# Layer 1's feed-forward in a small vision tower: scores and values of two steps in one run each, value products by column halves

## The chip, the cores and the metric
One core of a Trainium2 chip runs the whole program. The metric is the device time of one execution in microseconds, the median of the runs.

## What is computed
The reference is a tower of two layers over 32 images of 3 x 256 x 256: a tokenizer (16 x 16 patches, 256 tokens of 256 features per image), then per layer an attention and a feed-forward, each behind a layer norm and added to the stream. The change lies in layer 1's feed-forward, which is itself a small attention with experts. For every image, with 4 heads `n`, 4 experts `e`, 64 features per head and s = 256 tokens:

```
sx = x @ hl_w.T + hl_b                          # 4 heads of 64 features
q[n,e] = sx[n] @ wq[n,e].T ; k[n] = sx[n] @ wk[n].T ; v[n] = sx[n] @ wv[n].T
att[n,e] = softmax(q[n,e] @ k[n].T * 8 + causal)
out[n,e] = att[n,e] @ v[n]
gs[n] = softmax over e of (out[n,:] flattened @ gate_w[n].T + gate_b[n])
mixed[n] = sum over e of gs[n,e] * out[n,e]
h = layernorm(mixed + resid) ; y = layernorm(relu(h @ fc1.T + b1) @ fc2.T + b2 + h)
result = y * softmax over heads of (y @ fgate_w.T)
```

Everything is float32.

## The kernel before
The stages (tokenizer, layer 0 attention, layer 0 feed-forward, layer 1 attention, layer 1 feed-forward) run one after the other over all images; the 32 images' streams `H` stay on the chip. All matrix products write one of 8 PSUM banks of 512 columns, handed out in turn by `bank()`; every product goes through the helper `mm` (L113), so in the profile nearly all have that line and are told apart by their tiles. Each product shows there as two passes, each with a weight load (PEld).

In the last stage `A` holds wq and wk multiplied into each other, so that scores need `g = A.T sx` and `sx` alone; `WV` holds wv beside four small blocks, one per expert, that carry the values through `gate_w`, and `ones_row` adds a column of ones to each block, which yields the softmax's denominator. An image goes through pieces:

- `prep` 0 to 5: normalize and transpose (`ex`, `exT`), `sx` (weights `hl`), `g` for head pairs 0 and 1 (products `sx,A`, 64 x 64 tiles of the array, two heads side by side), the values `ev` (weights `WV`), a tile for the output `eo`.
- six score steps k (head pair k // 3, part k % 3). `scores` makes two products `g,sx` of 512 columns, one per head, on 64-row tiles; `weights` adds the triangular mask to the bank (VectorE, L825) and writes the exponential into `et` (ScalarE, L828).
- six value steps. For a head and a half of the tokens, `values` multiplies `et` (128 x 128 as weights) with the head's 84 columns of `ev` for each expert, into one bank of 4 x 84 columns, and ScalarE copies it to `eo` (L839). In the second half of the tokens there are two products per expert.
- `post` 0 to 13: reciprocal of the denominators, gate logits, softmax over the experts, `eo` times `gate` on GpSimd (L888), the sum over the experts (`two`, `er`, VectorE L893 to L896), a norm (`ss` on VectorE, `hv` by a power on GpSimd L844 and L845, the product L906), transposes into `fxT`, `fc1`, `fc2` and `centre`, a second norm (`ey`), transposes into `foT`, `fo_w`, the gate over heads (`fgate`) and `fout`, which is sent to memory.

A time step `t` enters an image every 6 steps, so up to five images are in hand. Within a step the order written is: scores, posts, preps, mask and exponential, values. So TensorE's stream has, in each of the six steps of a lap, one score run of 4 passes, then products on the full array, then one value run of 16 passes. Each engine takes its queue in order; waits between the queues are semaphores.

## Time and profile before
| | |
|---|---|
| median of 3 runs | 2424.4 us (2422.5 to 2426.04) |
| the profiled execution | 2421.16 us, span 2419.4 us |
| mean granted TensorE clock | 0.983 |
| busy share of the span | PE 97%, PEld 70%, DVE 57%, ACT 35%, POOL 21% |
| starts of `eo` on POOL (L888), images 3 to 30 | 30.03 to 30.05 us apart |

PE is TensorE's matrix passes, PEld its weight loads, DVE VectorE, ACT ScalarE, POOL GpSimd. Passes overlap in the array, so their lengths are modelled; the distance between starts is the better measure. An idle time in brackets behind a row names what ended it.

### The profile page before, as it was taken

What the parts mean: (1) busy time and instruction counts of PE and PEld (TensorE: products, weight loads), DVE (VectorE), ACT (ScalarE), POOL (GpSimd) and SP (SyncE); (2) the same over time, 40 slices, a digit from 0 to 9 for tenths busy, and PEclk for the clock granted to TensorE, in tenths of its full rate; (3) what the DMA queues carried; (4) which work ended last, traced back from release to release, by engine and by line L of the source; (5) the groups of instructions that cost most, each with busy time, mean ns of one, the idle gap of its engine ahead of it and who ended that gap; (6) DMA issues with size and microseconds to landing.
All of it is one profiled execution on the core that took longest, in us unless ns stands there. A gap on an engine that the chain in (4) does not pass through costs nothing.

```text
span 2419.4 us, 30697 instructions
## 1 busy us (share of the span) xinstructions
PE 2337.0 (97%) x12062; PEld 1681.9 (70%) x12062; DVE 1387.6 (57%) x3769; ACT 850.2 (35%) x1543; POOL 517.2 (21%) x461
## 2 busy tenths in 40 slices
PE   8999999999979999999999999999999999999995
PEld 6885666666656776766676667777777777777774
DVE  2435333333366665455465555777777777777775
ACT  0003222222202122144344444555555555555552
POOL 0002122221122121143233102222222222222222
PEclk9999999999989999999899999999999999999997
DMA  7420000000010000000000000000000000000000
GB/s 281 146 98 1 0 1 1 0 1 1 0 38 1 1 1 1 1 1 1 1 1 1 1 1 1 10 10 10 10 10 10 10 10 10 10 10 10 10 10 19
DMA packets 25895, 44.32 MB, mean 18 GB/s; under 512 B 1936, under 2 KB 11408, under 8 KB 25360
## 3 DMA queue, kind: packets, MB, share of 16 engines
q1 hardware_dynamic: 23872, 36.00, 4.3%
q10 hardware_dynamic: 1872, 6.29, 0.7%
q8 instruction: 97, 1.59, 0.3%
q14 instruction: 54, 0.44, 0.1%
HBM read 33.90 MB, written 8.39 MB: 17 GB/s over the span
## 4 chain that ended last, share of the span: by engine, by line
PE 91%; DVE 4%; ACT 1%; DMA 1%; POOL 1%; issue 1%; SPq 0%; DVEq 0%; ACTq 0%; POOLq 0%
PE bank L113 86%; PE bank L481 2%; PE bank L186 1%; DMA patch<-in_patches_dram 1%; PE bank L946 1%; POOL hv L845 1%; PE bank L947 1%; ACT bxT L191 0%; DVE cx L172 0%; POOL eo L888 0%; ACT et L828 0%; PE bank L539 0%; PE bank L586 0%; DVE bank L825 0%; DVE fout L960 0%
## 5 line engine op out<-in xcount | busy, mean ns | idle before, releaser
L113 PEld LDWEIGHTS bank<-ev,et 128*128 128x128 f32 x3072 | 361.2, 192 | 28.5 <-issue 11.7
L113 PE MATMUL bank<-ev,et 128*128 128x84 f32 x3072 | 373.7, 275 | 0.0
L828 ACT ACTIVATE et<-bank 128x512 f32<-128x512 f32 x384 | 222.3, 597 | 345.1 <-DVE bank L825 344.4
L113 PE MATMUL bank<-g,sx 64*128 64x512 f32 x768 | 216.9, 641 | 0.0
L825 DVE TENSOR_TENSOR bank<-bank,w_tri 128x256 f32<-128x256 f32 (+1 forms) x384 | 185.4, 514 | 52.2 <-PE bank L113 52.2
L888 POOL TENSOR_TENSOR eo<-eo,gate 128x2048 f32<-128x2048 f32 x32 | 115.8, 3620 | 394.5 <-DVE gate L886 394.5
L113 PE MATMUL bank<-w_tokW,patch 128*128 128x256 f32 x768 | 168.7, 384 | 11.9 <-DMA patch<-in_patches_dram 11.8
L113 PEld LDWEIGHTS bank<-w_tokW,patch 128*128 128x128 f32 x768 | 147.9, 193 | 32.3 <-DMA patch<-in_patches_dram 12.3
L113 PE MATMUL bank<-bxT,w_wuv 128*128 128x512 f32 x320 | 146.9, 598 | 4.9 <-ACT bxT L191 4.8
L839 ACT COPY eo<-bank 128x336 f32<-128x336 f32 x256 | 109.9, 444 | 98.5 <-PE bank L113 97.6
L332 DVE TENSOR_TENSOR bv<-bank,rows_b 128x512 f32<-128x512 f32 x64 | 44.3, 692 | 157.9 <-PE bank L113 157.9
L113 PE MATMUL bank<-sx,A 64*64 64x256 f32 x1024 | 124.3, 383 | 0.6 <-ACT sx L771 0.6
L113 PE MATMUL bank<-w_w,hT 128*128 128x256 f32 x512 | 115.8, 380 | 0.0
L113 PE MATMUL bank<-xsel,w_w 128*128 128x512 f32 x256 | 114.2, 600 | 0.0
L113 PE MATMUL bank<-w_wo,gT 128*128 128x256 f32 x512 | 113.1, 380 | 0.0
L113 PE MATMUL bank<-attn,bv 128*128 128x256 f32 x512 | 113.1, 380 | 0.0
L113 PE MATMUL bank<-w_wuv,bxT 128*128 128x512 f32 x256 | 112.5, 593 | 0.0
L113 PEld LDWEIGHTS bank<-attn,bv 128*128 128x128 f32 x512 | 97.5, 191 | 19.4 <-issue 7.2
L113 PEld LDWEIGHTS bank<-w_wo,gT 128*128 128x128 f32 x512 | 97.5, 191 | 13.0
L845 POOL TENSOR_TENSOR hv<-hv,minus_half 128x8 f32<-128x8 f32 x64 | 104.7, 1636 | 5.3
L113 PEld LDWEIGHTS bank<-bxT,w_wuv 128*128 128x128 f32 x320 | 59.5, 190 | 65.1 <-issue 53.6
L113 PEld LDWEIGHTS bank<-w_w,hT 128*128 128x128 f32 x512 | 95.7, 191 | 12.2 <-issue 0.5
(238 smaller groups left out, 3974.3 us busy)
## 6 DMA issues: line engine op xcount, KB each, us to landing
patch<-in_patches_dram SPq DMA_DIRECT2D x16, 1536.0 KB, 6.4
out_dram<-fout SPq DMA_DIRECT2D x32, 256.0 KB, 2.1
w_w<-in_w_dram ACTq DMA_DIRECT2D x2, 1024.0 KB, 13.4
w_wuv<-in_wuv_dram ACTq DMA_DIRECT2D x1, 1152.0 KB, 13.7
w_tokW<-in_tokW_dram ACTq DMA_DIRECT2D x1, 768.0 KB, 7.5
w_wo<-in_wo_dram ACTq DMA_DIRECT2D x1, 512.0 KB, 16.3
rows_b<-in_rows_b_dram ACTq DMA_DIRECT2D x1, 384.5 KB, 14.8
rows_e<-in_rows_e_dram ACTq DMA_DIRECT2D x1, 296.0 KB, 4.1
```

The lines of the kernel that those rows point to most:

```text
L113: nc.tensor.matmul(o, lhsT, rhs, start=first, stop=last)
L186: nc.tensor.transpose(p[:, o : o + P], x[:, c, k * P : (k + 1) * P], ident)
L332: nc.vector.tensor_tensor(v, p, row_b("b_v"), ALU.add)
L481: nc.tensor.transpose(p[:, o : o + P], x[:, c, k * P : (k + 1) * P], ident)
L825: nc.vector.tensor_tensor(own, own, over(tri, [P, n_e, P], 1), ALU.add)
L828: nc.scalar.activation(t.rearrange("p e n -> p (e n)"), p, AF.Exp)
L839: nc.scalar.copy(im.o[:, c * NH + n, 0 : NE * VC], p[:, 0 : NE * VC])
L845: nc.gpsimd.tensor_tensor(v, v, minus_half, ALU.pow)
L888: nc.gpsimd.tensor_tensor(im.by_e, im.by_e, over(im.gate, [P, NC * NH, NE, HD], 3), ALU.mult)
L946: nc.tensor.matmul(p[:, 0 : P + NH], im.fT[:, 0, s], fo_w[:, 0, :], start=True, stop=True)
L947: nc.tensor.matmul(p[:, P : 2 * P + NH], im.fT[:, 1, s], fo_w[:, 1, :], start=False, stop=True, skip_group_check=True,)
```

## The change
Four things change, all in this stage.

`A` becomes block-diagonal over the two heads of a pair (128 x 128 with zeros off the blocks), and the products `sx,A` run on the full array, one for two heads.

The columns of a head's values are laid out as experts 0 and 1's gate blocks, the 64 values, experts 2 and 3's blocks, so that an expert needs only a window of 74, 69, 69 or 74 columns of the 84. A value product is made by column halves: 64 of the 128 weight columns each, into partitions 0 to 63 and 64 to 127 of the bank.

The steps are paired. On even steps the scores of steps k and k+1 follow each other (8 passes); on odd steps a third of an image's values (64 half-width passes). Mask and exponential of k come on the even step, those of k+1 on the odd one.

The posts are spread over 19 steps instead of 14 in a table, and an image takes 34 steps instead of 29. Where `eo` was read as one view over four experts it is now two views of two, so the reciprocal, the gate logits and GpSimd's product are two instructions each; GpSimd's are half as long in elements.

```diff
-    VC = HD + NE * (NE + 1)
-    OC = NE * (VC + NE + 1)
+    EC = NE + 1
+    VC = NE * EC + HD
+    TAKE = ((0, 2 * EC + HD), (EC, EC + HD), (2 * EC, EC + HD), (2 * EC, 2 * EC + HD))
+    OC = sum(w for _, w in TAKE)
...
-    A = pwe.tile([P, 2, NE, HD], F32, name="A")
+    A = pwe.tile([P, 2, NE, P], F32, name="A")
...
                     for e in range(2):
-                        for h in range(2):
-                            s = slice(h * HD, (h + 1) * HD)
-                            mm(p[s, e * N : (e + 1) * N], A[s, hp, 2 * j + e, :], im.sx[s, hp, :])
+                        mm(p[:, e * N : (e + 1) * N], A[:, hp, 2 * j + e, :], im.sx[:, hp, :])
...
         def values(im, j):
-            hp, part = j // 3, j % 3
-            for n, c in (((2 * hp, 0), (2 * hp + 1, 0)), ((2 * hp, 1),), ((2 * hp + 1, 1),))[part]:
+            for n, c in (((0, 0), (1, 0), (0, 1)), ((1, 1), (2, 0), (3, 0)), ((2, 1), (3, 1)))[j]:
                 p = bank()
                 t0, t1 = im.t[n]
+                o = 0
                 for e in range(NE):
+                    x, w = n * VC + TAKE[e][0], TAKE[e][1]
                     for m in range(c + 1):
                         t = t1[:, e, :] if m else t0[:, e, c * P : (c + 1) * P]
-                        mm(p[:, e * VC : (e + 1) * VC], t, im.v[:, m, n * VC : (n + 1) * VC], m == 0, m == c)
-                nc.scalar.copy(im.o[:, c * NH + n, 0 : NE * VC], p[:, 0 : NE * VC])
+                        for q in (slice(0, HD), slice(HD, P)):
+                            mm(p[q, o : o + w], t[:, q], im.v[:, m, x : x + w], m == 0, m == c)
+                    o += w
+                nc.scalar.copy(im.o[:, c * NH + n, 0:OC], p[:, 0:OC])
...
-                nc.gpsimd.tensor_tensor(
-                    im.by_e, im.by_e, over(im.gate, [P, NC * NH, NE, HD], 3), ALU.mult
-                )
+                im.mix = [expert_pair(im, k, MIX, HD) for k in range(2)]
+                for k in range(2):
+                    nc.gpsimd.tensor_tensor(
+                        im.mix[k], im.mix[k], over(im.gate[:, :, 2 * k : 2 * k + 2], [P, NC * NH, 2, HD], 3), ALU.mult
+                    )
...
-        PREP, POST = 6, 15
+        SCORES, VALUES = 6, 9
+        POST = {15: 0, 16: 1, 17: 2, 19: 3, 20: 4, 21: 5, 22: 6, 23: 7, 27: 8, 28: 9, 29: 10, 30: 11, 32: 12, 33: 13}
...
+            if t % 2:
+                weigh()
+            else:
+                for b, i in active:
+                    if SCORES <= i < SCORES + 6:
+                        scores(images[b], i - SCORES)
+                        scores(images[b], i - SCORES + 1)
             for b, i in active:
-                if i >= POST:
-                    post(b, images[b], i - POST)
+                if i in POST:
+                    post(b, images[b], POST[i])
             for b, i in active:
-                if i < PREP:
-                    prep(b, images[b], i)
...
+                prep(b, images[b], i)
+            if t % 2:
+                for b, i in active:
+                    if VALUES <= i < VALUES + 6:
+                        values(images[b], (i - VALUES) // 2)
+            else:
+                weigh()
```

The framework reorders instructions within a queue when the program is built. In the built program of the changed kernel a lap (6 steps) stands in this order on each queue, by tiles; several images are mixed:

```
PE    fc1; values, third 2; scores 0 and 1; transposes of ey; A, pair 1; transposes of ex; WV;
      values, third 3; scores 2 and 3; fo_w; hl (sx); fc2 and centre; values, third 1;
      scores 4 and 5; transposes of er; A, pair 0
DVE   mask 0 (2), mask 1 (2); copy g; ex (2); ev (2); rden (2), lg, good, mask 2, good, lg, mask 2;
      gate sum, mask 3, gate softmax with mask 3 and the fgate copies between, gate last product;
      fgate, fout (8); two; ey; er, er; ss; mask 4; good; ey x hv; mask 4; ss; mask 5 (2); good;
      er x hv; junk (2); copy g
ACT   exp 0 (2), exp 1, foT, exp 1; copy g; copy exT; eo (2); exp 2 (2), exp 3, gate exp, exp 3,
      fgate exp; sx (2); eo (2); square of ey; eo; square of er; exp 4 (2), exp 5, fxT, copy g,
      exp 5; hx; eo (3)
POOL  eo x gate in two halves; hv of ey (2); hv of er (2)
```

`two` waits for POOL's second half, `ey x hv` and `er x hv` for `hv`, and `fc1` for `fxT`.

More of the change, by code (lines that the diff above doesn't have):

```diff
@@ L372, in vit_tower @@
     LOW, HIGH, MOST = 1e-28, 1e28, 1e37
-    VC = HD + NE * (NE + 1)
-    OC = NE * (VC + NE + 1)
+    EC = NE + 1
+    VC = NE * EC + HD
+    TAKE = ((0, 2 * EC + HD), (EC, EC + HD), (2 * EC, EC + HD), (2 * EC, 2 * EC + HD))
+    OC = sum(w for _, w in TAKE)
+    starts = [sum(w for _, w in TAKE[:e]) for e in range(NE)]
+    OWN = [starts[e] + (0, EC, 2 * EC + HD, 3 * EC + HD)[e] - TAKE[e][0] for e in range(NE)]
+    MIX = [starts[e] + 2 * EC - TAKE[e][0] for e in range(NE)]
     right_e, right_d, passing = ExitStack(), ExitStack(), ExitStack()
@@ L438, in prepare @@
             nc.vector.tensor_scalar(wo1[:, k, :], wo1[:, k, :], col("ln_w", k), None, ALU.mult)
-        for t in (WV, ones_row, fc2):
+        for t in (A, WV, ones_row, fc2):
             nc.gpsimd.memset(t, 0.0)
-        nc.gpsimd.memset(
-            ones_row.rearrange("p (n x) -> p n x", n=NH)[:, :, HD:VC]
-            .rearrange("p n (e x) -> p n e x", e=NE)[:, :, :, NE : NE + 1], 1.0,
-        )
+        for n in range(NH):
+            for o in (NE, EC + NE, 2 * EC + HD + NE, 3 * EC + HD + NE):
+                nc.gpsimd.memset(ones_row[:, n * VC + o : n * VC + o + 1], 1.0)
         nc.vector.tensor_copy(fo_w[:, 0, 0:P], ident)
@@ L460, in prepare @@
                 mm(pv[s, hp * 16 : hp * 16 + 16], wv_o[s, hp, :], gw_d[s, hp, :])
-        nc.scalar.mul(A.rearrange("p h e d -> p (h e d)"), pa, math.sqrt(HD))
         for i in range(2):
             s = slice(i * HD, (i + 1) * HD)
+            nc.scalar.mul(A[s, :, :, s], pa[s].rearrange("p (h e d) -> p h e d", h=2, e=NE), math.sqrt(HD))
             nc.vector.tensor_copy(fc2[s, s], f2[s, :])
@@ L467, in prepare @@
                 w = WV[s, hp, i * VC : (i + 1) * VC]
-                nc.vector.tensor_copy(w[:, 0:HD], wv_i[s, hp, :])
-                nc.vector.tensor_copy(
-                    w[:, HD:].rearrange("p (e x) -> p e x", e=NE)[:, :, 0:NE],
-                    pv[s, hp * 16 : hp * 16 + 16].rearrange("p (e x) -> p e x", e=NE),
-                )
+                nc.vector.tensor_copy(w[:, 2 * EC : 2 * EC + HD], wv_i[s, hp, :])
+                for k, o in enumerate((0, 2 * EC + HD)):
+                    nc.vector.tensor_copy(
+                        w[:, o : o + 2 * EC].rearrange("p (e x) -> p e x", e=2)[:, :, 0:NE],
+                        pv[s, hp * 16 + k * 8 : hp * 16 + k * 8 + 8].rearrange("p (e x) -> p e x", e=2),
+                    )
     def feature_major(x):
@@ L756, in vit_tower, with __init__ @@
         class Image:
-            pass
+            def __init__(self):
+                self.p, self.t = {}, {}
         G8 = [P, NC * NH, HD]
@@ L763, in prep @@
                 im.xT = features(p2, b)
-            if i == 1:
+            if i == 2:
                 im.sx = p2.tile([P, 2, N], F32, name="sx")
@@ L774, in prep @@
                 im.g = p2.tile([P, 2, NE, N], F32, name="g")
-            if i in (2, 3):
-                hp = i - 2
+            if i in (4, 6):
+                hp = i // 2 - 2
                 for j in range(2):
@@ L779, in prep @@
                     for e in range(2):
-                        for h in range(2):
-                            s = slice(h * HD, (h + 1) * HD)
-                            mm(p[s, e * N : (e + 1) * N], A[s, hp, 2 * j + e, :], im.sx[s, hp, :])
+                        mm(p[:, e * N : (e + 1) * N], A[:, hp, 2 * j + e, :], im.sx[:, hp, :])
                     copy_split(j, im.g[:, hp, 2 * j : 2 * j + 2, :].rearrange("p e n -> p (e n)"), p)
-            if i == 4:
+            if i == 7:
                 im.v = p2.tile([P, NC, NH * VC], F32, name="ev")
@@ L796, in prep @@
                 )
-            if i == 5:
-                im.o = p2.tile([P, NC * NH, OC], F32, name="eo")
+                im.o = p2.tile([P, NC * NH, 360], F32, name="eo")
         def scores(im, k):
@@ L804, in scores @@
             if part == 0:
-                im.t = getattr(im, "t", {})
                 for h in range(2):
@@ L809, in scores @@
                     )
-            im.p = []
+            im.p[k] = []
             for h in range(2):
@@ L816, in scores @@
                     mm(p, im.sx[s, hp, P:N], im.g[s, hp, :, P:N])
-                im.p.append(p)
+                im.p[k].append(p)
         def weights(im, k):
@@ L822, in weights @@
             for h in range(2):
-                p, n_e = im.p[h], 4 if part == 2 else 2
+                p, n_e = im.p[k][h], 4 if part == 2 else 2
                 own = p.rearrange("p (e n) -> p e n", e=n_e)[:, :, 0:P]
@@ L865, in squares, with expert_pair @@
             return sq
+        def expert_pair(im, k, at, w):
+            x, step = at[2 * k], at[2 * k + 1] - at[2 * k]
+            return im.o[:, :, x : x + 2 * step].rearrange("p g (e x) -> p g e x", e=2)[:, :, :, 0:w]
         def post(b, im, i):
             if i == 0:
-                by_e = im.o.rearrange("p g (e x) -> p g e x", e=NE)
                 im.rden = spool.tile([P, NC * NH, NE], F32, name="rden")
-                nc.vector.reciprocal(im.rden, by_e[:, :, :, HD + NE])
+                lg = spool.tile([P, NC * NH, NE, NE], F32, name="lg")
+                own = [expert_pair(im, k, OWN, EC) for k in range(2)]
+                for k in range(2):
+                    nc.vector.reciprocal(im.rden[:, :, 2 * k : 2 * k + 2], own[k][:, :, :, NE])
                 nc.vector.scalar_tensor_tensor(good, im.rden, 1.0 / LOW, good, ALU.is_le, ALU.mult)
                 nc.vector.scalar_tensor_tensor(good, im.rden, 1.0 / HIGH, good, ALU.is_ge, ALU.mult)
-                lg = spool.tile([P, NC * NH, NE, NE], F32, name="lg")
-                nc.vector.tensor_tensor(
-                    lg, by_e[:, :, :, HD : HD + NE], over(im.rden, [P, NC * NH, NE, NE], 3), ALU.mult
-                )
+                for k in range(2):
+                    e = slice(2 * k, 2 * k + 2)
+                    nc.vector.tensor_tensor(
+                        lg[:, :, e, :], own[k][:, :, :, 0:NE], over(im.rden[:, :, e], [P, NC * NH, 2, NE], 3), ALU.mult
+                    )
                 im.gate = spool.tile([P, NC * NH, NE], F32, name="gate")
@@ L886, in post @@
                 nc.vector.tensor_tensor(im.gate, im.gate, im.rden, ALU.mult)
-                im.by_e = im.o[:, :, 0 : NE * VC].rearrange("p g (e x) -> p g e x", e=NE)[:, :, :, 0:HD]
-                nc.gpsimd.tensor_tensor(
-                    im.by_e, im.by_e, over(im.gate, [P, NC * NH, NE, HD], 3), ALU.mult
-                )
+                im.mix = [expert_pair(im, k, MIX, HD) for k in range(2)]
+                for k in range(2):
+                    nc.gpsimd.tensor_tensor(
+                        im.mix[k], im.mix[k], over(im.gate[:, :, 2 * k : 2 * k + 2], [P, NC * NH, 2, HD], 3), ALU.mult
+                    )
             if i == 3:
                 two = p1.tile([P, NC * NH, 2, HD], F32, name="two")
-                nc.vector.tensor_tensor(two, im.by_e[:, :, 0:2, :], im.by_e[:, :, 2:4, :], ALU.add)
+                nc.vector.tensor_tensor(two, im.mix[0], im.mix[1], ALU.add)
                 im.r = p2.tile(G8, F32, name="er")
@@ L968, in vit_tower, with weigh @@
         images = [Image() for _ in range(B)]
-        PREP, POST = 6, 15
-        for t in range(6 * (B - 1) + POST + 14):
-            active = [(b, t - 6 * b) for b in range(B) if 0 <= t - 6 * b < POST + 14]
+        SCORES, VALUES = 6, 9
+        POST = {15: 0, 16: 1, 17: 2, 19: 3, 20: 4, 21: 5, 22: 6, 23: 7, 27: 8, 28: 9, 29: 10, 30: 11, 32: 12, 33: 13}
+        for t in range(6 * (B - 1) + 34):
+            active = [(b, t - 6 * b) for b in range(B) if 0 <= t - 6 * b < 34]
+            def weigh():
+                for b, i in active:
+                    if SCORES <= i < SCORES + 6:
+                        weights(images[b], i - SCORES)
+            if t % 2:
+                weigh()
+            else:
+                for b, i in active:
+                    if SCORES <= i < SCORES + 6:
+                        scores(images[b], i - SCORES)
+                        scores(images[b], i - SCORES + 1)
             for b, i in active:
-                if PREP <= i < PREP + 6:
-                    scores(images[b], i - PREP)
+                if i in POST:
+                    post(b, images[b], POST[i])
             for b, i in active:
-                if i >= POST:
-                    post(b, images[b], i - POST)
-            for b, i in active:
-                if i < PREP:
-                    prep(b, images[b], i)
-            for b, i in active:
-                if PREP <= i < PREP + 6:
-                    weights(images[b], i - PREP)
-            for b, i in active:
-                if PREP + 3 <= i < PREP + 9:
-                    values(images[b], i - PREP - 3)
+                prep(b, images[b], i)
+            if t % 2:
+                for b, i in active:
+                    if VALUES <= i < VALUES + 6:
+                        values(images[b], (i - VALUES) // 2)
+            else:
+                weigh()
         n_bad = p1.tile([P, 2], F32, name="n_bad")
```

## The prediction
> **What bounds the kernel now.** I read the page first, then the busy time of each engine over one lap of layer 1's feed-forward (one image enters per lap), then the timeline of TensorE, and last the waits of the other queues. The lap is read off POOL's `eo` instruction (L888), which starts at 1881.36, 1911.40 and 1941.43 us: 30.04 us, 27 times alike.

> ```profile
> PE 2337.0 (97%) x12062; PEld 1681.9 (70%) x12062; DVE 1387.6 (57%) x3769; ACT 850.2 (35%) x1543; POOL 517.2 (21%) x461
> ...
> 1881.36:1911.40 30.04, 30.04 (x210) 21.97 (x206) 21.97 (x60) 15.48 (x33) 7.38 (x6) 1.00 0.03 9
> ```

> The second line is a lap: span, then PE, PEld, DVE, ACT, POOL busy. TensorE has no idle moment; VectorE has 8 us to spare. So today what TensorE's stream costs is what a lap costs, and the queues of the others have slack. Whether they keep it is the question.

> ```profile
> 1905.18 2.02 PE L113 MATMUL bank<-ev,et 128*128 128x84 f32 x16
> 1907.13 1.13 PE L113 MATMUL bank<-g,sx 64*128 64x512 f32 x4
> 1908.19 0.49 PE L946 MATMUL bank<-fo_w,foT 128*128 128x132 f32 x2
> 1908.52 0.39 PE L947 MATMUL bank<-fo_w,foT 128*128 128x132 f32 x2
> 1908.74 0.39 PE L946 MATMUL bank<-fo_w,foT 128*128 128x132 f32 x2
> ...
> 1909.72 1.94 PE L113 MATMUL bank<-sx,A 64*64 64x256 f32 x16
> 1911.60 2.02 PE L113 MATMUL bank<-ev,et 128*128 128x84 f32 x16
> ```

> Starts matter here, not lengths. Each product is two passes. Two `fo_w` passes of 132 columns (1908.52 to 1908.74) take 0.225 us, 0.112 each. A value pass of 84 columns takes 0.112 too (1905.18 to 1907.13: 15 x 0.112, its own stream of 0.07, and a gap), so it is paced by loading 128 weight columns, not by its columns. Two score passes on the two row halves start 7 ns apart and stream 0.427; the pairs of `sx,A` take 0.216. A change of tile shape empties the array: 0.13 us of gap before the scores, 0.10 after, and the next weight load (0.10) is then uncovered.

> **The change, TensorE alone.** Values: 96 passes x 0.112 = 10.7 us become 96 pairs of half-width passes. The nearest rows for one half are those of the weight preparation, 64-column loads and 64-column streams:

> ```profile
> 766.34 0.73 PE L113 MATMUL bank<-w_wk_o,w_wq_o 64*64 64x64 f32 x10
> 766.85 0.24 PE L113 MATMUL bank<-w_gw_d,w_wv_o 64*64 64x16 f32 x2
> 766.91 0.56 PE L113 MATMUL bank<-w_wk_o,w_wq_o 64*64 64x64 f32 x8
> ```

> Read instruction by instruction, a pass starts there every 0.058 us; a load takes 0.054 and begins 2 ns after the stream of the same tile. The columns, at 0.216/256 per column, give 0.058 for 69 and 0.062 for 74. If both halves load and stream together, as the two tiles of `sx,A` do, a pair takes 0.062: 6.0 us, 4.7 saved. If loads take turns, 2 x 0.056 = 0.112: nothing saved; if load and stream of the halves also exclude each other, 0.125. I take 0.062, the row of two tiles side by side. What no row shows is two tiles sharing all 128 rows.
> [...]

> Shapes: before, a lap has 16 changes of shape; after, `A` is block-diagonal and full (16 passes x 0.216 = 3.5 us, as the 16 pairs before), and scores and values come in three runs each, so there are 9 changes. Uncovered gaps fall from 3.4 to 1.8 us. TensorE's own work per lap: 30.0 - 4.7 - 1.6 = 23.7 to 24.2 us.

> **The change, the other queues.** In the built order of the changed kernel the queues close a loop that has to be run once per lap. I add it from rows of one lap (start to next start).
> 1. TensorE from `fc1` to the end of the third value run. `fc1` 0.97; values 2.0; scores of two steps 0.10 + 4 x 0.427 = 1.81; eight transposes x 0.109 = 0.87; `A` 1.73; `WV` 8 x 0.143 = 1.14; values 2.0; four gaps 0.65: 11.2 us.
> 2. ScalarE's `eo` copy, 0.24 after the last pass, 0.40 (286 columns; 0.444 for 336): 0.65.
> 3. VectorE from the reciprocals to the last `gate` product: before, 1907.70 to 1911.25 = 3.55 with two 0.34 additions of the mask inside; after, two of 0.61 come in beside them, and the reciprocal and the product behind it are two instructions each; some of that fills bubbles between small dependent steps: 4.6 (4.8 if none does).
> 4. GpSimd's product `eo` by `gate`: 0.15 to start, 3.62 as one, 1.8 to 2.05 per half as two: 4.0.
> 5. VectorE: `two` 1.13, `ey` 0.60, `er` 0.72 and 0.61, `ss` 0.60; GpSimd's `hv` 0.2 + 1.64 with two hand-overs, 2.0; then `ey` x `hv`, a mask addition 0.94, `ss` 0.60, the first mask addition of step 5, 0.69: 7.9.
> 6. ScalarE: that step's exponential 0.50, then `fxT` 0.76, behind it in the queue though its bank has long been full: 1.3; then `fc1`.
> Sum 29.7 us; with the bounds of steps 3 and 4 29.4 to 30.1. So TensorE no longer sets the lap: the loop does, and it is hardly shorter than 30.04.

> ```profile
> 1911.40 3.62 POOL L888 TENSOR_TENSOR eo<-eo,gate 128x2048 f32<-128x2048 f32 x1 [11.31 <-DVE gate L886]
> 1912.70 2.34 DVE L858 TENSOR_TENSOR fgate<-fgate,sm_m 128x8 f32<-128x8 f32 x1
> 1917.76 1.21 DVE L893 TENSOR_TENSOR two<-eo 128x1024 f32<-128x1024 f32 x1
> ```

> Today `two` comes 2.7 us after GpSimd has finished; in the new order VectorE reaches it first and stands there. The tiny `fgate` product that now waits out GpSimd (2.34 us) gets in after the first half instead and then has the eight `fout` rows (1.5 us) inside the second half's time: no cost. If it has to wait for both halves, 1.6 us per lap more.

> TensorE meanwhile does in steps 2 to 6 (18.5 us): scores, `fo_w`, `hl`, `fc2`, values, scores, transposes, `A`: 13.0 us. It is idle 5.5 us in front of `fc1`, once per lap. Today it never is, in this stage. What such an idle spell does:

> ```profile
> 1416.27:1419.68 3.41, 1.17 (x6) 0.75 (x7) 3.19 (x13) 0.59 (x1) 1.31 (x2) 1.00 0.00 0
> 1419.68:1423.09 3.41, 3.17 (x8) 1.97 (x6) 0.00 (x0) 0.21 (x1) 0.00 (x0) 0.50 0.00 0
> 1423.09:1426.50 3.41, 3.09 (x30) 2.03 (x32) 1.39 (x3) 1.45 (x4) 0.00 (x0) 1.00 0.00 0
> ...
> 2372.00:2375.41 3.41, 2.09 (x19) 2.12 (x20) 1.46 (x3) 0.78 (x1) 1.92 (x3) 1.00 0.00 0
> ...
> 2382.24:2385.65 3.41, 0.00 (x0) 0.00 (x0) 1.25 (x2) 0.63 (x1) 2.72 (x1) 1.00 0.17 56
> 2385.65:2389.07 3.42, 0.00 (x0) 0.00 (x0) 1.85 (x4) 0.00 (x0) 2.08 (x2) 0.50 0.00 0
> ```

> The number behind POOL's is the granted clock. All six drops of the clock in this trace fall on one grid of 3.41 us. A stretch of it with 1.17 us of TensorE work, after only 2.44 us of idling, is followed by half clock; one with 2.09 is not; full clock returns after a stretch with 3.17. An idle spell of 5.5 us falls on two or three stretches, one of which keeps at most 0.7 us of work: half clock in every lap. It then holds from `fc1` to the end of the first well-filled stretch, 2.4 to 5.6 us, mean 3.8, and the work in it takes twice as long: 1.2 to 2.8 us lost, 1.9 in the mean, inside step 1 and so on the loop.
> [...]

> Lap: 29.7 + 1.9 = 31.6 to 31.7, 1.65 more than 30.04. The 31 laps count as 29 full ones (the two at each end are shorter): +48 us. Memsets and copies of the preparation lie in a stage where GpSimd is 21% busy: 0 to +1; the longer spacing of the last images' pieces: -5 to +5, taken as 0. From the profiled execution, 2421.2 us (span 2419.4), to 2469; the median of the runs lies 3.2 above the profiled one: 2472.

> **The rivals.**
> *The idle spell does not halve the clock* (faster). If steps 3 and 5 were shorter, so that less than about 1.5 us of idling fell in any stretch, or the half clock missed the loop, the lap would be the loop's 29.4 to 29.9 at most: -18 to -4 us, 2406 to 2420; the point where it decides is an idle spell of about 3 us (two stretches with 1.5 each). For it: VectorE and ScalarE are only 73% and 52% busy. Against: the loop's waits on GpSimd (4.0 and 2.0) are fixed lengths. Should the loop vanish entirely, TensorE's 24.2 would give 2421 - 29 x 5.8 = 2253; no row supports it.
> *The two halves take turns* (slower still). The two value runs of step 1 are 64 pairs; 0.112 instead of 0.062 adds 3.2 us per lap, +93: 2565; half of that, if only issue is slower, 2518. For it: no row has tiles sharing rows. Against: `sx,A` and `g,sx`, 7 ns apart.
> *The pieces balance out* (no change): 0.05.

> **Numbers.** Forecast 0.61 (2450 to 2495), halves in turn or slowed 0.21 (to 2565), faster 0.13, no change 0.05. Range 2432 to 2568, which takes in the turns and leaves out the faster and the unchanged cases. A measurement tells 0.2%, about 5 us.

> **What would show it.** After: starts of the `eo` product 31.6 us apart; an idle spell of 5 to 6 us before `fc1`, released by ScalarE's `fxT`; mean granted clock 0.90 to 0.95 over a lap; value pairs 0.062 apart; `two` starting as GpSimd ends. Wrong if TensorE stays above 97% busy with a lap under 29, or if value pairs take over 0.1.

## The result and the profile after

The changed kernel takes 2465.2 us (median of 4 runs, 2464.6 to 2466.4) against 2425.1 us (2422.5 to 2426.0) on the same chip: ratio 1.0168, 95% interval 1.0150 to 1.0185, so 40 us slower. The forecast was 2472, the range 2432 to 2568. The profiled execution took 2464.6 us, its span is 2462.8 us, 43.4 more than the span before.

The page first: the share of each engine, the granted clock in 40 slices, the chain that ended last by engine, and two of the costliest groups (busy time and mean ns; then the idle time before them and what ended it).

```profile
PE 2213.8 (90%) x14622; PEld 1597.7 (65%) x14622; DVE 1365.9 (55%) x3837; ACT 850.5 (35%) x1544; POOL 522.1 (21%) x509
...
PEclk9999999999989999999899998989888989898986
...
PE 73%; DVE 15%; POOL 7%; ACT 3%; issue 1%; DMA 1%; SPq 0%; DVEq 0%; ACTq 0%; POOLq 0%
...
L906 POOL TENSOR_TENSOR eo<-eo,gate 128x1024 f32<-128x1024 f32 x64 | 122.0, 1927 | 590.1 <-DVE fgate L860 513.7
...
L113 PE MATMUL bank<-fxT,w_fc 128*128 128x512 f32 x64 | 64.5, 1110 | 164.4 <-ACT fxT L928 164.4
```

TensorE does less (2214 us busy instead of 2337) and the kernel is slower. It stands still 164 us in front of `fc1`, a wait that the kernel before did not have in its laps, and from the start of this stage (slice 24 of 40) more than half of the clock digits are 8. The mean lap (starts of the `eo` product, images 3 to 30) is 31.61 us, where it was 30.04; the median is 31.66, by which one expectation below reckons. Here is TensorE around one `fc1` (start, length, instruction, tiles; in brackets the idle time before it and its releaser), then the clock's own stretches over the same time (span, then PE, PEld, DVE, ACT, POOL busy and the granted clock).

```profile
1881.83 2.21 PE L113 MATMUL bank<-ev,et 128*64 128x74 f32 x64
1883.96 1.99 PE L113 MATMUL bank<-g,sx 64*128 64x512 f32 x8
...
1895.04 1.89 PE L113 MATMUL bank<-sx,A 128*128 128x256 f32 x8
1902.35 2.08 PE L113 MATMUL bank<-fxT,w_fc 128*128 128x512 f32 x2 [5.42 <-ACT fxT L928]
1904.35 2.94 PE L113 MATMUL bank<-ev,et 128*64 128x74 f32 x64
1907.22 1.99 PE L113 MATMUL bank<-g,sx 64*128 64x512 f32 x8
```

```profile
1892.27:1895.69 3.42, 3.42 (x29) 2.03 (x26) 3.16 (x7) 0.85 (x2) 0.68 (x1) 1.00 0.23 77
1895.69:1899.10 3.41, 1.24 (x6) 0.76 (x4) 1.78 (x5) 1.18 (x3) 1.83 (x2) 1.00 0.00 0
1899.10:1902.52 3.42, 0.17 (x1) 0.17 (x2) 2.66 (x7) 2.09 (x4) 1.83 (x2) 0.50 0.00 0
1902.52:1905.93 3.41, 3.41 (x28) 1.91 (x30) 2.50 (x6) 1.43 (x3) 0.00 (x0) 0.50 0.00 0
1905.93:1909.34 3.41, 3.41 (x52) 2.10 (x51) 0.86 (x3) 1.68 (x4) 0.00 (x0) 1.00 0.02 5
```

```profile
1889.14 3.81 POOL L906 TENSOR_TENSOR eo<-eo,gate 128x1024 f32<-128x1024 f32 x2 [18.41 <-DVE fgate L860]
```

```profile
1889.74 1.36 DVE L867 TENSOR_TENSOR fgate<-fgate,sm_m 128x8 f32<-128x8 f32 x1
1891.13 1.63 DVE L978 SCALAR_TENSOR_TENSOR fout<-bank,fgate,h 128x64 f32<-128x64 f32 x8
1892.98 1.23 DVE L911 TENSOR_TENSOR two<-eo 128x1024 f32<-128x1024 f32 x1 [0.23 <-POOL eo L906]
...
1898.77 0.69 DVE L924 TENSOR_TENSOR ey<-ey,hv 128x512 f32<-128x512 f32 x1 [1.63 <-POOL hv L854]
```

GpSimd's two halves end at 1892.95 and `two` starts at 1892.98. `fgate` lasts until the first half, 1.93 us from 1889.14, is done (1.36 us, to 1891.10, where the same product on `gate` takes 0.19), and the eight `fout` rows fit into the second.

### The profile page after: what moved, and what is told of

Its sections match the earlier page's. It is cut to its first block, busy times and chain, and to the rows that moved or that the text cites. A ratio compares the mean times of both kernels' runs of the same rounds, so it can differ in the third digit from the quotient of the medians.

```text
span 2462.8 us, 35995 instructions
## 1 busy us (share of the span) xinstructions
PE 2213.8 (90%) x14622; PEld 1597.7 (65%) x14622; DVE 1365.9 (55%) x3837; ACT 850.5 (35%) x1544; POOL 522.1 (21%) x509
## 3 DMA queue, kind: packets, MB, share of 16 engines
q8 instruction: 117, 1.92, 0.3%
## 4 chain that ended last, share of the span: by engine, by line
PE 73%; DVE 15%; POOL 7%; ACT 3%; issue 1%; DMA 1%; SPq 0%; DVEq 0%; ACTq 0%; POOLq 0%
PE bank L113 69%; POOL eo L906 5%; DVE bank L831 4%; POOL hv L854 2%; DVE ss L918 2%; DVE two L911 2%; PE bank L488 2%; PE bank L186 1%; DVE ey L924 1%; DVE er L914 1%; ACT fxT L928 1%; DVE ey L949 1%; ACT et L834 1%; DVE er L913 1%; DMA patch<-in_patches_dram 0%
## 5 line engine op out<-in xcount | busy, mean ns | idle before, releaser
L113 PEld LDWEIGHTS bank<-ev,et 128*64 128x64 f32 x6144 | 230.3, 154 | 57.9 <-DVE junk L938 43.6
L906 POOL TENSOR_TENSOR eo<-eo,gate 128x1024 f32<-128x1024 f32 x64 | 122.0, 1927 | 590.1 <-DVE fgate L860 513.7
L113 PE MATMUL bank<-ev,et 128*64 128x74 f32 (+1 forms) x6144 | 245.6, 245 | 1.6 <-ACT et L834 1.6
L113 PE MATMUL bank<-fxT,w_fc 128*128 128x512 f32 x64 | 64.5, 1110 | 164.4 <-ACT fxT L928 164.4
L113 PE MATMUL bank<-g,sx 64*128 64x512 f32 x768 | 191.8, 617 | 1.8 <-ACT g L191 1.7
L113 PE MATMUL bank<-w_tokW,patch 128*128 128x256 f32 x768 | 168.9, 384 | 12.5 <-DMA patch<-in_patches_dram 12.5
L113 PEld LDWEIGHTS bank<-w_tokW,patch 128*128 128x128 f32 x768 | 147.9, 193 | 33.1 <-DMA patch<-in_patches_dram 12.5
L848 ACT COPY eo<-bank 128x286 f32<-128x286 f32 x256 | 100.8, 396 | 163.4 <-PE bank L113 158.3
L113 PE MATMUL bank<-bxT,w_wuv 128*128 128x512 f32 x320 | 146.9, 598 | 4.9 <-ACT bxT L191 4.8
L113 PEld LDWEIGHTS bank<-fxT,w_fc 128*128 128x128 f32 x64 | 15.6, 303 | 176.7 <-ACT fxT L928 176.7
L113 PE MATMUL bank<-sx,A 128*128 128x256 f32 x512 | 121.9, 381 | 1.1 <-ACT sx L781 0.6
L113 PE MATMUL bank<-w_w,hT 128*128 128x256 f32 x512 | 115.8, 379 | 0.0
L113 PE MATMUL bank<-attn,bv 128*128 128x256 f32 x512 | 113.1, 379 | 0.0
L113 PE MATMUL bank<-w_wo,gT 128*128 128x256 f32 x512 | 113.1, 379 | 0.0
L113 PE MATMUL bank<-xsel,w_w 128*128 128x512 f32 x256 | 112.9, 594 | 0.0
L113 PE MATMUL bank<-w_wuv,bxT 128*128 128x512 f32 x256 | 112.5, 592 | 0.0
L113 PEld LDWEIGHTS bank<-attn,bv 128*128 128x128 f32 x512 | 97.3, 190 | 19.6 <-issue 7.2
L113 PEld LDWEIGHTS bank<-w_wo,gT 128*128 128x128 f32 x512 | 97.3, 190 | 13.2
```

Of the source, the lines that this page charges most:

```text
L113: nc.tensor.matmul(o, lhsT, rhs, start=first, stop=last)
L848: nc.scalar.copy(im.o[:, c * NH + n, 0:OC], p[:, 0:OC])
L906: nc.gpsimd.tensor_tensor(im.mix[k], im.mix[k], over(im.gate[:, :, 2 * k : 2 * k + 2], [P, NC * NH, 2, HD], 3), ALU.mult)
```

## Experiments

The theory on trial: the halves are worth having; the new order makes a loop through VectorE, GpSimd and ScalarE that is about as long as a lap was before; TensorE's idle time in that loop halves the clock, which makes the lap longer still. The rivals: the halves themselves take turns, or the idle time costs nothing beyond itself, or a single place (GpSimd's power, the place of `fc1`) explains it all. Times of each group stand against the kernel before on the same chip, 2423.8 to 2424.7 us in the median.

**Full-width passes in the new order.** Each pair of column halves is one pass on the full array again.

```
-                        for q in (slice(0, HD), slice(HD, P)):
-                            mm(p[q, o : o + w], t[:, q], im.v[:, m, x : x + w], m == 0, m == c)
+                        mm(p[:, o : o + w], t, im.v[:, m, x : x + w], m == 0, m == c)
```

> The changed kernel with one part undone: value products at full width again (128 weight columns, windows of 69 and 74 columns), all else as changed. Theory (queues' loop sets the lap, and two value runs lie on it; halves side by side pay 0.062 us a pair): a full-width pass is paced by its 128-column load, 0.112 us, so the two runs on the loop grow by 64 x 0.05 = 3.2 us, the idle spell in front of fc1 shrinks by the third run's 1.6 us to about 3.8, the clock still drops in most laps: lap 34 to 34.5 us, total 2540 to 2560 us. Rival (column halves bring nothing, a pair costs what a full-width pass costs): 2465 us, within 10.

Measured 2643.0 us (2641.6 to 2649.5), ratio 1.0913 (1.0895 to 1.0931): slower as expected, by far more than expected. So the halves are no cause of the loss. The lap settles at 37.55 us; the clock is half for 13.65 us of each, four stretches, where the changed kernel has one or two:

```profile
1934.18:1937.59 3.41, 1.03 (x5) 0.57 (x3) 2.13 (x5) 1.67 (x5) 1.45 (x1) 1.00 0.00 0
1937.59:1941.00 3.41, 2.68 (x7) 1.65 (x7) 2.05 (x6) 2.24 (x5) 1.83 (x2) 0.50 0.00 0
1941.00:1944.42 3.42, 3.42 (x18) 3.42 (x17) 1.09 (x3) 0.52 (x2) 0.00 (x0) 0.50 0.00 0
1944.42:1947.83 3.41, 3.41 (x15) 3.01 (x16) 0.00 (x0) 0.80 (x2) 0.00 (x0) 0.50 0.02 5
1947.83:1951.24 3.41, 3.41 (x10) 1.14 (x7) 1.06 (x3) 1.09 (x2) 0.00 (x0) 0.50 0.00 0
1951.24:1954.66 3.42, 3.42 (x24) 3.16 (x23) 1.73 (x6) 2.82 (x5) 0.00 (x0) 1.00 0.00 0
```

Two stretches that show TensorE busy throughout do not bring the clock back. Value passes fill the first of them (3.42 us) and 2.64 us of the second: 32 passes take 6.88 us to the next start, 0.215 each, where 74 columns would stream in 0.125 by 0.216 per 256 columns, doubled (an estimate). Weight loads are busy for 3.42 and 3.01 us of these two; the stretch that does bring the clock back holds no value pass, and its loads are busy for 1.14. The kernel without the power, below, shows a stretch filled with half-width pairs, loads busy for 3.33, that does bring it back. What tells these stretches apart for the clock, no run shows.

**The halves in the old order.** Column halves, windows and the block-diagonal `A` stay; the order of steps is that of before (one score run and one value run per step), with the products on `A` in `prep` 2 and 3.

```
-        SCORES, VALUES = 6, 9
-        POST = {15: 0, 16: 1, 17: 2, 19: 3, 20: 4, 21: 5, 22: 6, 23: 7, 27: 8, 28: 9, 29: 10, 30: 11, 32: 12, 33: 13}
+        PREP, POST = 6, 15
...
-            if i in (4, 6):
-                hp = i // 2 - 2
+            if i in (2, 3):
+                hp = i - 2
```

> Column halves, the 69 and 74 column windows and the block-diagonal A, but the old order of pieces: six score steps, six value steps, posts one step apart. Theory (the loss is the new order's loop and the clock it costs; the halves save 4.7 us of TensorE's work per lap and the old order has the slack to use much of it): lap 26.5 to 28 us, idle under 3.5 us per lap and split, clock full, total 2330 to 2365 us. Rival (halves bring nothing, or twelve changes of shape with half-width tiles eat them): 2420 us or more.

Measured 2344.1 us (2341.6 to 2346.4), ratio 0.9669 (0.9653 to 0.9685), lap 27.24, with a granted clock of 1.00 over the lap from 1900 us. TensorE's timeline has a wait here too, but a short one:

```profile
1922.69 0.66 PE L488 MATMUL bank<-ident,ey 128*128 128x128 f32 x4
1924.83 1.99 PE L113 MATMUL bank<-sx,A 128*128 128x256 f32 x8 [1.48 <-ACT sx L781]
1926.75 1.22 PE L113 MATMUL bank<-ev,et 128*64 128x74 f32 x32
1927.90 1.13 PE L113 MATMUL bank<-g,sx 64*128 64x512 f32 x4
```

A value run of 16 pairs takes 1.15 us to the next start. So the arithmetic part of the change gains 3.3%, and the order takes it away and more.

**Full-width passes in the old order.** The same kernel with the first edit.

> The old order again (one score run and one value run in each step), with the windows and the block-diagonal A, but each value product as one pass on the full array instead of two column halves. If the halves are what the old order gained, TensorE's busy time per lap goes from 25.76 to about 30.3 us (six value runs of 16 passes at 0.112 instead of 16 pairs at 0.065, 0.76 each), TensorE is again the bound, its idle 1.49 us before the products on A vanish, and the lap is 30.3 to 30.7: 2430 to 2445 us, no faster than the kernel before, whose 84 columns cost a load-paced pass no more than 69 or 74. If A on the full array and the closer pieces are what gained, the lap stays under 29: below 2395 us.

Measured 2392.3 us (2391.0 to 2392.7), ratio 0.9872 (0.9855 to 0.9888): between the two expectations. TensorE is the bound, as expected, but at 29.07 us, not 30.3:

```profile
1918.47 0.66 PE L488 MATMUL bank<-ident,ey 128*128 128x128 f32 x4
1918.96 1.89 PE L113 MATMUL bank<-sx,A 128*128 128x256 f32 x8
1920.69 1.90 PE L113 MATMUL bank<-ev,et 128*128 128x74 f32 x16
1922.53 1.13 PE L113 MATMUL bank<-g,sx 64*128 64x512 f32 x4
```

The estimate took the pairs' runs as they stood, gaps included, and added 0.76 for each; a run of 16 full passes takes 1.84, that is 0.69 more than 1.15, and it stands without a change of shape behind the full-array passes in front of it: `sx,A` takes 1.73 us to the start of the run here, 1.92 to that of the pairs in the old order. So against the kernel before, 0.97 of a lap is gained without the halves, and the halves add 1.83: TensorE's 29.07 falls to 25.76 busy, and 1.49 of that goes into the wait for `sx`. The windows have no visible part in the 0.97: a run of 16 passes takes 1.84 with 84 columns too (before, 1899.82 to 1901.66). About 0.70 is saved around the two groups of `sx,A`, which no longer change the tile shape. These are the rows of one of them before; from the transposes to the scores behind the value run, at 1907.13, it is 4.41 us, and 4.06 here:

```profile
1902.72 0.66 PE L481 MATMUL bank<-ident,ey 128*128 128x128 f32 x4
1903.31 1.94 PE L113 MATMUL bank<-sx,A 64*64 64x256 f32 x16
```

Another 0.24 is saved from `fc1` to the value run behind `WV` (2.34 before, 2.10 here), where the tiles are alike in both kernels; no run shows why.

**The new order, kept warm.** Eight products into a bank that nobody reads stand in front of `fc1`.

```
+                q = bank()
+                for _ in range(8):
+                    mm(q[:, 0:336], ident, ones_row[:, 0:336])
```

> The changed kernel plus eight products of ones_row by the identity (16 passes of 336 columns, 4.5 us) in front of fc1, whose result nobody reads: work added to fill TensorE's idle spell. Theory (the idle spell of 5.4 us halves the clock, and the half clock then costs about 1.4 us of each lap): clock full in this stage, fc1 0.43 us a pass instead of 1.0, lap 29.7 to 30.0, total 2410 to 2430 us: added work makes it faster. Rival (only the waits cost, the half clock is hidden or costs nothing): 2465 us, or more by what the added passes push back.

Measured 2402.7 us (2402.6 to 2404.2), ratio 0.9916 (0.9899 to 0.9932): added work makes the changed kernel some 60 us faster, a little below the expected 2410 to 2430.

```profile
1897.56 1.89 PE L113 MATMUL bank<-sx,A 128*128 128x256 f32 x8
1899.29 4.68 PE L113 MATMUL bank<-ones_row,ident 128*128 128x336 f32 x16
1904.87 1.12 PE L113 MATMUL bank<-fxT,w_fc 128*128 128x512 f32 x2 [0.90 <-ACT fxT L928]
```

The granted clock over the lap from 1900 us is 1.00; the lap is 29.54, so half clock cost the changed kernel 31.61 - 29.54 = 2.07 us per lap, where the expectation had 1.4. `fc1` still waits for `fxT`: 29.54 is the loop's length at full clock, 2.30 more than the 27.24 of the old order.

**Full-width passes, kept warm** (the first edit, with five such products).

> Full-width value products in the new order, as in e3_fullwidth, plus five products of ones_row by the identity (10 passes of 336 columns, 2.8 us) in front of fc1 whose result nobody reads. e3 took 37.56 us a lap with the clock low for 13.65 of them. Theory (that excess over the forecast 34.3 is clock, because passes paced by their weight loads do not count as work enough to bring the clock back; the width itself costs 1.5 to 3.2 us of the 29.54 us loop): clock full, lap 31 to 32.8, total 2445 to 2500 us. Rival (full-width values really cost 6 us a lap in this order): lap 35 to 37, total 2570 us or more.

Measured 2463.2 us (2460.9 to 2465.7), ratio 1.0158 (1.0142 to 1.0173), lap 31.38. So of the 37.55 of the first experiment 6.2 us were half clock. A run of 32 full passes takes 3.62 us here (1909.97 to 1913.59), a run of 32 pairs 2.13: 1.49 a run, 4.5 for the three of a lap. The lap grows by only 1.84, because this edit also changed the built order: `fc1` to the end of the third value run is 2.78 longer than in the warm run (13.92 against 11.14), but on VectorE two mask additions moved ahead, and from `two` to the exponential of step 5 it is 0.93 shorter (7.12 against 8.05). The first experiment has the same order as this one.

**Without GpSimd's power.** It stands twice in a lap, once in the loop.

```
-            nc.gpsimd.tensor_tensor(v, v, minus_half, ALU.pow)
```

> The changed kernel with GpSimd's power left out (hv is the mean square itself, not its inverse root; the output is not the reference's). Theory (the loop ss, hv, ey x hv, mask of step 5, exponential, fxT, fc1 sets the lap): one 1.64 us power lies on it, so the lap is 1.4 to 1.7 us shorter and the idle spell falls from 5.4 to about 3.8 us: 2415 to 2425 us. Rival (GpSimd, 21% busy, is off the path; the lap is TensorE's work at the lower clock): 2465 us, within 5.

Measured 2431.1 us (2427.0 to 2434.6), ratio 1.0028 (1.0016 to 1.0039): less gain than expected, although the idle time fell to 3.80 per lap as reckoned. The lap is 30.72, nearly the same every time, with two stretches of half clock in each:

```profile
1918.61:1922.02 3.41, 0.51 (x3) 0.10 (x1) 3.41 (x8) 2.16 (x4) 0.40 (x2) 1.00 0.00 0
1922.02:1925.43 3.41, 2.53 (x10) 1.03 (x12) 2.79 (x8) 2.22 (x5) 0.00 (x0) 0.50 0.02 5
1925.43:1928.85 3.42, 3.42 (x60) 3.33 (x58) 0.00 (x0) 1.06 (x3) 0.00 (x0) 0.50 0.00 0
1928.85:1932.26 3.41, 3.41 (x21) 2.02 (x18) 1.63 (x4) 2.12 (x5) 0.00 (x0) 1.00 0.01 2
```

The third of these holds nothing but half-width value passes, and the clock comes back behind it. The same kernel kept warm by five products:

> GpSimd's power left out, as in e8b_nopower (output not the reference's), plus the five unread products in front of fc1. e8b's lap was 30.72 us, only 0.94 less than the changed kernel's, with the clock low for 6.83 us of each. Theory (the power lies on the loop with its full 1.64 us, and e8b gave back part of it to the clock): lap 27.7 to 28.1 against 29.54 with full clock and power, total 2345 to 2362 us. Rival (only half of the power lies on the path): lap 28.6 or more, 2375 us or more.

Measured 2349.4 us (2348.6 to 2349.8), ratio 0.9691 (0.9676 to 0.9705), lap 27.90: 1.64 less than 29.54, the whole length of one power. At full clock the loop gives the whole of this part back; with the half clock only 0.89 of 1.64 arrives (31.61 to 30.72).

**`fc1` two half-steps later.** `23: 7` becomes `25: 7` in `POST`.

> The changed kernel with one number changed: fc1 (post 7) at step 25 instead of 23, two half-steps later, so that fxT need not be ready where TensorE now stands. Theory (fc1 behind fxT behind the exponential of step 5 is where the loop closes): TensorE next waits in front of the second value run for the exponentials of step 4, a shorter hold, so the lap falls by 0.5 to 1.2 us: 2425 to 2450 us, idle before fc1 gone. Rival (the hold at fc1 is only where the wait shows, the loop closes anyway): 2465 us, within 5.

Measured 2436.9 us (2436.1 to 2439.0), ratio 1.0053 (1.0037 to 1.0068). The lap is 30.72. `fc1` waits no more, and others do:

```profile
PE bank L113 <- ACT et L834: 47.7, 26, 1.8
PE bank L113 <- ACT g L191: 42.5, 26, 2.1
```

```profile
1917.57:1920.98 3.41, 1.07 (x28) 0.76 (x24) 2.90 (x6) 1.28 (x3) 1.59 (x3) 1.00 0.00 0
1920.98:1924.39 3.41, 2.08 (x6) 0.51 (x6) 2.66 (x7) 2.44 (x6) 0.69 (x1) 0.50 0.00 0
1924.39:1927.81 3.42, 3.42 (x10) 1.82 (x11) 1.37 (x4) 1.86 (x4) 0.00 (x0) 0.50 0.01 2
```

(The first pair of lines is the waits of TensorE: total us, times, longest.) Two waits of 1.84 and 1.61 us take the place of one of 5.42. The first and part of the second fall into one stretch, which keeps 1.07 us of work, and the clock halves all the same.

**The best order tried.** The old order once more, with the products on `A` at `prep` 3 and 4 and the values `ev` at 5, so that `sx` is ready sooner than it is asked for.

```
-            if i in (2, 3):
-                hp = i - 2
+            if i in (3, 4):
+                hp = (3, 4).index(i)
```

> Column halves in the old order, as in e4_oldorder, with the products sx,A one step later (steps 3 and 4 of prep instead of 2 and 3) and the values ev at step 5. In e4 TensorE's only idle spell, 1.48 us a lap, stands in front of sx,A, released by ScalarE's sx, which is queued behind exponentials. Theory (that wait is all that is left to gain): idle under 1.1 us, lap 26.8 to 27.0, 2329 to 2338 us. Rival (the wait moves on to the next wait of that queue): 2344 us, within 4.

Measured 2324.9 us (2322.5 to 2326.1), ratio 0.9588 (0.9575 to 0.9601): the fastest here, 4.1% below the kernel before and a little under the expected 2329 to 2338. The lap is 26.78; the wait for `sx` is gone and one for `exT`, 1.07 us, is what remains:

```profile
1906.47 1.99 PE L113 MATMUL bank<-exT,w_hl 128*128 128x256 f32 x8 [1.07 <-ACT exT L495]
```

## Why the prediction was right, by its steps

The lap, taken apart by the runs:

| kernel | lap, us | step |
|---|---|---|
| before | 30.04 | |
| old order, `A` full, windows | 29.07 | -0.97 |
| the same with halves | 27.24 | -1.83 |
| new order, at full clock | 29.54 | +2.30 |
| new order, as changed | 31.61 | +2.07 |

*TensorE alone.* A pair at 0.062: a run of 32 pairs takes 2.13 us with its gap of about 0.13, so 0.0625. Predicted 4.7 saved on the values, measured 4.5. TensorE's own work per lap, predicted at 23.7 to 24.2, is 23.9 in the warm run (29.54 less 0.93 idle and 4.68 of unread products). The rival in which halves take turns is out. Loads that take turns, at half of 0.112 each, would have made the 64 half-width passes of a run 3.6 us long (an estimate).

*The loop.* Predicted 29.7, measured 29.54 in the warm run, step by step in its trace: `fc1` to the end of the third value run 11.14 (11.2), from there to GpSimd's start 5.18 (0.65 + 4.6), GpSimd to `two` 3.85 (4.0), `two` to the exponential of step 5 8.05 (7.9), that exponential to `fc1` 1.31 (1.3). No step is off by more than 0.15.

```profile
1875.34 1.13 PE L113 MATMUL bank<-fxT,w_fc 128*128 128x512 f32 x2 [0.90 <-ACT fxT L928]
1886.48 1.99 PE L113 MATMUL bank<-g,sx 64*128 64x512 f32 x8
1891.66 3.81 POOL L906 TENSOR_TENSOR eo<-eo,gate 128x1024 f32<-128x1024 f32 x2 [16.28 <-DVE fgate L860]
1895.51 1.23 DVE L911 TENSOR_TENSOR two<-eo 128x1024 f32<-128x1024 f32 x1 [0.23 <-POOL eo L906]
1903.56 0.60 ACT L834 ACTIVATE et<-bank 128x512 f32<-128x512 f32 x1 [0.59 <-DVE bank L831]
1904.87 1.12 PE L113 MATMUL bank<-fxT,w_fc 128*128 128x512 f32 x2 [0.90 <-ACT fxT L928]
```

*Idle time.* Predicted 5.5 us before `fc1`, once a lap, released by `fxT`; measured 5.43 in the mean, all of it there.

*The half clock.* Predicted 1.9 us lost, between 1.2 and 2.8, inside step 1; measured 2.07. It lies where it was placed: in the changed kernel `fc1` to the end of the third value run takes 12.60 to 14.07 us, in the mean of four laps 13.20, instead of 11.14, and each other step of the loop is within 0.02 of the warm run. The granted clock over four laps is 0.91, within the 0.90 to 0.95 named. What was thought a fresh draw of the grid's position in each lap is not one: from image to image the laps repeat 31.67, 31.22, 30.97, 32.44, together 126.3 us, which is 37 times 3.413.

*Lap and total.* Predicted 31.65, measured 31.61; that agreement is partly luck, since the loop came out 0.16 short and the clock 0.17 long. The total came out lower: from the first `eo` product to the last the trace grew by 46.0 (predicted 48); the first one starts 8.8 earlier than before, and the end behind the last one is 6.2 longer. The ends were taken as nothing within 5; they are -2.6. So the span grew by 43.4. The medians differ by 40.1, since the profiled run of before lies 3.9 under the median of its group and the one of after 0.7. The forecast had 48 for the span and 3.2 for the offset of the median; 4.6 less of the one and 2.5 of the other are the 7 us between forecast and result.

*The range.* Its upper end, 2568, was there for halves that take turns. With 0.0625 measured, nothing near it was possible. The faster rival (idle time without half clock) named 2406 to 2420; the warm run, which is that case, shows 2402.7.

Where the expectations of the full-width kernel, of the warm one and of the one without the power failed, it was mainly at one point: the half clock was priced as a mean over positions of the grid, and it is neither constant nor such a mean. Against the same kernel at full clock it costs 2.07 us a lap in the changed kernel, 2.82 without the power and 6.2 with full-width passes. The full-width kernel had its width too high as well, 3.2 for the 1.84 that it costs at full clock.

## What to carry over

Here passes paced by a 128-column weight load (0.112 us) were cut into column halves that ran side by side (0.0625 a pair); that is worth having where TensorE is the bound, and the order around it has to be chosen so that TensorE stays the bound. Before pieces are moved, add up the loop through the other queues in the built order: here it was 29.5 us where TensorE needed 24, and it could be read off before the run. Where TensorE must wait, look at the work left in each stretch of the granted clock, 3.413 us in these traces, and not at the length of the wait alone: two waits of 1.84 and 1.61 us close together left 1.07 us of work in one and the clock halved, as after the 1.24 that a wait of 5.42 left. Unread products in the gap won back some 60 us here; the old order, where TensorE waits 1.49 us a lap, won more.

## What the runs showed of the hardware

- The four kernels with half clock in every lap settled on multiples of the clock's stretch of 3.413 us: a lap of 30.72 is 9 of them in two different kernels, one of 37.55 is 11, and four laps of the changed kernel are 37. Taking 1.64 us out of the loop and moving `fc1` both gave the same lap. Laps of 26.78, 27.24, 27.90 and 29.54 at full clock are 7.85, 7.98, 8.17 and 8.65 stretches.
- In the traces of before and after, from 20 us on, the 44 stretches at full clock that half clock followed show 0 to 1.55 us of TensorE work, and those that full clock followed 1.61 or more. In the rows above, 0.51 (without the power), 1.03 (full width) and 1.07 us (`fc1` later) were followed by half clock. The wait of 1.48 us in the old order left at least 1.93 of a stretch, and the clock of that lap is 1.00. At half clock, the stretches of before and after that half clock followed show up to 2.94 us busy and those that full clock followed 3.08 or more; in the first experiment two of 3.4 us, with 3.42 and 2.64 us of full-width value passes, were followed by half clock all the same.
- GpSimd's product in two halves takes 1.93 us each where the whole took 3.62: 0.2 us more in all, and VectorE's waiting `fgate` gets in between.
